# First attention block: a tile's values at the head of the following step, the residual behind the transposes, its bias three steps later

## The chip, the cores and the metric

One kernel runs on one core of one Trainium2 chip, as one launch. The metric is the device time of a launch in microseconds. All arithmetic is in float32. PE is the matrix engine, DVE, ACT and POOL are the vector, scalar and general engines, SP issues the DMAs. PE, DVE, ACT and POOL each take their instructions strictly in the order in which the program records them. The order on SP is set by the framework.

## What is computed

Four stages follow each other, each with a layer norm ahead of it and a residual around it: an attention block with windows of 64 keys (stage A, the one that is changed), two layers of local attention with gated FFNs (stage B), a gated attention unit (stage C) and a ternary linear layer. The input is 2 sequences of 2048 tokens with 256 features. Cut to the changed stage:

```python
def _L0_attn_ref(x, ...):            # 16 query heads, 4 key heads, 16 features a head
    h = _layernorm(x, g1, b1)
    q, k, v = heads(h @ Wq + bq), heads(h @ Wk + bk), heads(h @ Wv + bv)
    q, k = _rope(q), _rope(k)
    scores = einsum(q, k) / sqrt(16)
    valid = (col <= row) & (row - col < 64)
    attn = softmax(where(valid, scores, -1e9))
    out = einsum(attn, v)
    x = x + (out @ Wo + bo)
    h2 = _layernorm(x, g2, b2)
    return x + gelu(h2 @ Wf1 + bf1) @ Wf2 + bf2

x = x + _L0_attn_ref(_layernorm(x), ...)
```

The block gets a normalised x, and normalises it again. So each row has two scales from one variance: rs[0] gives the block's input, which is its residual y, and rs[1] gives the twice normalised rows h.

## The kernel before

The 4096 rows are 32 tiles of 128, and four tiles are a group (GT = 4, eight groups). Stage A is a pipeline over steps: in step s tile s is projected, tile s-1 gets its scores, the weights of tile s-2 are transposed and multiplied with the values, and tile s-3 is multiplied with Wo and added to its residual. A table (`at(step, what, ...)`) says which step does what for which tile or group, and `step_a` writes the instructions of a step in an order set by hand; every engine keeps that order.

In a full step PE does, in this order: the scores of tile s-1 (L446, 64 small matmuls), the projection of tile s (L380), a piece of the FFN of an earlier group (`fill(0)`: L552 for hidden columns, L563 for output tiles), the transposes of the rotated queries and keys of tile s (L427, L428), the transposes of the weights of tile s-2 (L476), the second FFN piece (`fill(1)`), the values of tile s-2 (L496) with their row sums (L503), the output of tile s-3 (L518), and, in two of four steps, the eight transposes of a group of normalised rows (`transposed`, L215, copied by ACT in L220). Steps without FFN pieces (up to step 7, and some at the end) have the transposes of the weights ahead of L427.

DVE follows: the mask is added to the scores in four pieces (L456, `mask(0)` to `mask(3)`), between them come the bias of the projection (L389), the cosine product (L411) and the sums of the rotation (L416, L421), then the row maxima (L465, two halves), the sums of the FFN output pieces (L570), statistics (L145, L146), normalised rows (L170 for the attention, L198 for the FFN and for the stage's result), the reciprocal of the row sums and the product (L512, L513, `take_values`), and the residual sum (L524, `add_output`). POOL copies the values of the tile to a padded array (L392), from which SP sends two DMAs to the arrays `vmid`; it makes the two sine products (L403, L406), subtracts the maxima (L466), raises variances to -1/2 (L161 for two scales at once, L137 for one) and adds bias rows (`add_rows`, L207). ACT makes the exponents (L469), copies transposes from PSUM (L433, L434, L436, L484, L220), makes y (L184) and applies gelu (L558).

The norm of group g is spread over steps: its x is loaded in step 4g-5, its statistics (`statistics_twice`) are made in step 4g-3, its `normalise` in step 4g-2. `normalise` writes h on DVE, then y on ACT (`normalised_once`), and adds bo to y on POOL. The FFN norm of a group (`prepare`) stands in step 4g+7. Each PSUM tile takes one of eight banks. `statistics_twice` also serves the rows of stage C.

The lines of the step that the change moves, as they stand:

```python
        if e:
            e.last_normalise()
        if a:
            a.values()
            a.take_values()
        if o:
            o.output()
            o.add_output()
        if q:
            q.exponents()
```

Here `a` is tile s-2, `o` tile s-3, `q` tile s-1, `p` tile s; `m` is the group in its `normalise`, `f` the one in `prepare`, `e` the one that is finished.

Of the kernel before, what the change touches and what calls it, by code (L numbers as in the profile page):

```python
# [12 lines left out]
ALU = mybir.AluOpType  # L13
# [8 lines left out]
GT = 4  # L22
# [23 lines left out]
def kernel(ctx: ExitStack, tc: tile.TileContext, I: dict, out: bass.AP):  # L46
    nc = tc.nc
    uid = [0]

    def T(pool, shape, tag, bufs=None):  # L50
        uid[0] += 1
        kw = {} if bufs is None else {"bufs": bufs}
        return pool.tile(shape, F32, tag=tag, name=f"{tag}_{uid[0]}", **kw)
# [18 lines left out]
    mhalf = T(const, [P, 2 * BH], "mhalf")  # L72
# [67 lines left out]
    def means_of(src):  # L140

        mv = T(small, [P, GT, 2], "mv")
        for t in range(GT):
            st = T(small, [P, 6], "st")
            nc.vector.bn_stats(st, src[:, t, :])  # L145
            nc.vector.bn_aggr(mv[:, t, :], st)  # L146
        return mv

    def statistics_twice(src):

        mv = means_of(src)
        ve = T(small, [P, 2, GT], "ve2")
        nc.vector.tensor_scalar_add(ve[:, 0, :], mv[:, :, 1], EPS)
        nc.vector.tensor_scalar(ve[:, 1, :], mv[:, :, 1], 1.0 + EPS, EPS * EPS, ALU.mult, ALU.add)
        rs = T(small, [P, 2, GT], "rs2")  # L160
        nc.gpsimd.tensor_tensor(  # L161
            rs, ve, mhalf[:, 0 : 2 * GT].rearrange("p (a b) -> p a b", a=2), ALU.pow
        )
        return mv, rs

    def normalised_twice(src, stats, dst):

        mv, rs = stats
        for t in range(GT):
            nc.vector.tensor_scalar(  # L170
                dst[:, t, :], src[:, t, :], mv[:, t, 0:1], rs[:, 1, t : t + 1], ALU.subtract, ALU.mult
            )

    def normalised_once(src, stats, dst, residual):

        mv, rs = stats
        scale = rs[:, 0, :]
        shift = T(small, [P, GT], "sh2")
        nc.vector.scalar_tensor_tensor(shift, mv[:, :, 0], -1.0, scale, ALU.mult, ALU.mult)
        if residual:  # L180
            scale = T(small, [P, GT], "sc2")
            nc.vector.tensor_scalar_add(scale, rs[:, 0, :], 1.0)
        for t in range(GT):
            nc.scalar.activation(  # L184
                dst[:, t, :], src[:, t, :], AF.Identity,
                bias=shift[:, t : t + 1], scale=scale[:, t : t + 1],
            )
# [17 lines left out]
    def add_rows(dst, rows):  # L205
        for t in range(GT):
            nc.gpsimd.tensor_add(dst[:, t, :], dst[:, t, :], rows(t))  # L207
# [18 lines left out]
    def load_qkv(l):  # L226
        w = {}
        w["wqkv"] = T(wB, [P, KC, 3 * BIN], "wqkvB")
        load(w["wqkv"], I["L0_ffn_wqkv"][l].rearrange("(k p) n -> p k n", p=P))
        return w  # L230

    def load_wo(l):
        w = {}
        w["wo"] = T(wB, [P, BIN // P, D], "woB")
        load(w["wo"], I["L0_ffn_wo"][l].rearrange("(k p) n -> p k n", p=P))
        return w
# [42 lines left out]
    class GroupA:  # L279
# [7 lines left out]
        def statistics(self):  # L287
            self.stats = statistics_twice(self.xg)

        def normalise(self):  # L290
            self.h = T(wa, [P, GT, D], "h", 1)
            normalised_twice(self.xg, self.stats, self.h)
            self.y = T(wa, [P, GT, D], f"y{self.g % 3}", 1)
            normalised_once(self.xg, self.stats, self.y, residual=False)
            add_rows(self.y, lambda t: boA)

        def to_features(self):
# [287 lines left out]
    def at(step, what, *args):  # L585
        steps.setdefault(step, {}).setdefault(what, []).append(args)
# [6 lines left out]
    for g in range(NG):  # L593
        at(GT * g - 5, "load", g)
        at(GT * g - 3, "statistics", g)
        at(GT * g - 2, "normalise", g)
        s = GT * (g + 1) + 3
        at(s - 1, "residual", g)
        at(s, "prepare", g)

        if g < NG - 1:
            for c in range(ADFF // P):
                at(s + 1 + c // 4, f"fill{c // 2 % 2}", g, "hidden", c)
            for tt in range(GT):
                at(s + 3 + tt // 2, f"fill{tt % 2}", g, "output", tt)
        at(s + 5, "finish", g)

    groups_a, tiles_a, ffns_a = {0: first_group}, {}, {}
    steps_a = steps

    def step_a(todo):
        p = a = q = o = n = m = f = e = None
        for (g,) in todo.get("load", ()):
            if g:
                groups_a[g] = GroupA(g)
        if "project" in todo:
            (t,) = todo["project"][0]
            if t == GT:
                weights.update({**load_qkv(0), **load_wo(0), **load_ffn(0)})
            p = tiles_a[t] = TileA(t, groups_a[t // GT])  # L620
        if "scores" in todo:
            q = tiles_a[todo["scores"][0][0]]
        if "attend" in todo:
            a = tiles_a[todo["attend"][0][0]]
        if "output" in todo:
            o = tiles_a.pop(todo["output"][0][0])
        for (g,) in todo.get("residual", ()):
            ffns_a[g] = FfnA(groups_a[g])
        if "statistics" in todo:
            n = groups_a[todo["statistics"][0][0]]  # L630
        if "normalise" in todo:
            m = groups_a[todo["normalise"][0][0]]
        if "prepare" in todo:
            f = ffns_a[todo["prepare"][0][0]]
        if "finish" in todo:
            e = ffns_a.pop(todo["finish"][0][0])

        def fill(place):

            rest = []  # L640
            for g, what, i in todo.get(f"fill{place}", ()):
                x = ffns_a[g]
                if what == "hidden":
                    rest.append(lambda x=x, i=i, r=x.hidden(i): x.take_hidden(i, r))
                else:
                    rest.append(lambda x=x, i=i, r=x.output(i): x.take_output(i, r))
            return rest

        if q:
            q.scores()  # L650
            q.mask(0)
            q.mask(1)
        if p:
            p.project()
            p.take()
        if q:
            q.mask(2)
        if p:
            p.rotate()
        if q:  # L660
            q.maxima(0)
            q.mask(3)
            q.maxima(1)
        pieces = fill(0)
        if a and not pieces:
            a.weights_to_keys()
            a.take_weights()
        for r in pieces:
            r()
        if n:  # L670
            n.statistics()
        if f:
            f.statistics()
        if e:
            e.last_statistics()
        if p:
            p.to_features()
            p.take_features()
        if a and pieces:
            a.weights_to_keys()  # L680
            a.take_weights()
        for r in fill(1):
            r()
        if m:
            m.normalise()
        if f:
            f.normalise()
        if e:
            e.last_normalise()
        if a:  # L690
            a.values()
            a.take_values()
        if o:
            o.output()
            o.add_output()
        if q:
            q.exponents()
        if m:
            m.to_features()
        if f:  # L700
            f.to_features()


    wC = Region(W_A, END)
# [16 lines left out]
    class RowsC:  # L721
# [5 lines left out]
        def statistics(self):  # L727
            self.stats = statistics_twice(self.R)
# [353 lines left out]
    class Ffn:  # L1082
# [45 lines left out]
        def residual(self):  # L1128
            Rg, w = self.Rg, self.w
            for tt in range(GT):  # L1130
                nc.gpsimd.tensor_add(Rg[:, tt, :], Rg[:, tt, :], w["b2"])
            if self.l == BL - 1:
                for tt in range(GT):
                    nc.gpsimd.tensor_add(Rg[:, tt, :], Rg[:, tt, :], self.xr[:, tt, :])
# [225 lines left out]
    head_c, bias = [rows[0].statistics, rows[0].normalise, rows[1].statistics], bias_c()  # L1360
# [3 lines left out]
    with tc.manual_schedule(engines=ENGINES):  # L1364
        for s in range(min(steps_a), JOINT + max(steps) + 1):
            if s in steps_a:
                step_a(steps_a[s])
            if GT < s < JOINT - 4:
                next(masks, None)
            if s == JOINT + s_a + 6:  # L1370
                nc.gpsimd.memset(hh[:, 5, :], 0.0)
            step_b(steps.get(s - JOINT, {}))
# [32 lines left out]
    class BatchC:  # L1405
# [14 lines left out]
        def rows(self, gl_):  # L1420
            return rows[self.b * GPS + gl_]
# [292 lines left out]
```

## Time and profile before

| | |
|---|---|
| median of 3 runs | 2669.41 us (2669.31 to 2669.52) |
| profiled execution | 2669.28 us, span 2667.1 us |
| PE busy | 2598.4 us (97%) |
| DVE busy | 1608.5 us (60%) |
| ACT busy | 1198.5 us (45%) |
| POOL busy | 992.6 us (37%) |
| granted PE clock | 0.991 of full speed |

The profile is one execution. An instruction's record has its engine, line, operation, the tiles it writes and reads, its start and length; an idle time before it is put down to the event that ended it. Matmuls are pipelined, so a busy PE need not be at its peak. Nearly every tile lies in one large array that the program calls `room`; a bank of PSUM is called `ps`. "Step 2" and the like below are steps of stage A; step 0 projects tile 0. Stage A takes the time up to about 510 us; its last group's FFN is mixed with the first steps of stage B.

### The profile page before, as it was taken

Reading aid. Unit: us, or ns where it says so; the run is one execution under the profiler, and the core shown is the slowest. Engines: PE = TensorE matmul, PEld = TensorE weight load, DVE = VectorE, ACT = ScalarE, POOL = GpSimd, SP = SyncE. Lnnn points to the kernel's source line nnn. Section 1 sums busy time; section 2 is a strip of 40 time slices with the busy share of each in tenths; the row PEclk is TensorE's granted clock in tenths of the full one; section 3 lists DMA queues with packets and bytes.
Section 4 is the critical chain, followed back from the end, with each engine's and each line's share of the span. In section 5 each row is a group of like instructions: output and inputs, shape, how many; then the busy total and the mean of one; then the engine's idle time right before and its main releaser. Section 6 shows DMA issues by size and latency. Waiting matters only on the chain.

```text
span 2667.1 us, 51195 instructions
## 1 busy us (share of the span) xinstructions
PE 2598.4 (97%) x20130; PEld 1644.4 (62%) x20130; DVE 1608.5 (60%) x4357; ACT 1198.5 (45%) x2505; POOL 992.6 (37%) x1221
## 2 busy tenths in 40 slices
PE   6899999999999999999999999999999999999998
PEld 4577777566666666666666666666544445445567
DVE  6777777468666666756766666674434344434344
ACT  3555555366666666646666666663510001500000
POOL 5655555445444444433644544442200001300011
PEclk8999999999999999999999999999999999999999
DMA  5011110111100011111211111101100000100000
GB/s 169 17 31 32 31 48 26 43 37 47 25 21 21 25 29 25 49 27 39 78 29 25 29 33 35 27 17 57 29 19 4 6 7 12 44 0 6 4 10 12
DMA packets 73166, 82.00 MB, mean 31 GB/s; under 512 B 18829, under 2 KB 57056, under 8 KB 72672
## 3 DMA queue, kind: packets, MB, share of 16 engines
q1 hardware_dynamic: 72928, 78.75, 10.6%
q8 instruction: 159, 2.61, 0.4%
q14 instruction: 79, 0.65, 0.1%
HBM read 44.20 MB, written 10.50 MB: 21 GB/s over the span
## 4 chain that ended last, share of the span: by engine, by line
PE 91%; DVE 5%; POOL 2%; DMA 1%; issue 1%; SPq 0%; ACT 0%; DVEq 0%; ACTq 0%; POOLq 0%
PE ps L1567 16%; PE ps L893 12%; PE ps L1147 10%; PE ps L1170 6%; PE ps L1491 4%; PE ps L552 4%; PE ps L563 4%; PE ps L1075 4%; PE ps L968 3%; PE ps L1046 3%; PE ps L1510 2%; PE ps L1479 2%; PE ps L949 2%; PE ps L1018 2%; PE ps L1469 2%; PE ps L476 2%
## 5 line engine op out<-in xcount | busy, mean ns | idle before, releaser
L1567 PE MATMUL ps<-room 128*128 128x512 f32 (+1 forms) x1152 | 463.2, 544 | 0.0
L893 PE MATMUL ps<-room 128*128 128x512 f32 x768 | 364.0, 610 | 0.0
L1567 PEld LDWEIGHTS ps<-room 128*128 128x128 f32 x1152 | 217.8, 189 | 221.9 <-issue 214.7
L999 ACT ACTIVATE room<-room,shift,rn 128x192 f32<-128x192 f32 x512 | 275.5, 543 | 79.6 <-DVE shift L987 78.7
L914 POOL TENSOR_TENSOR room<-room 128x256 f32<-128x256 f32 x128 | 115.8, 905 | 473.6 <-ACT room L905 472.0
L1147 PE MATMUL ps<-room 128*128 128x512 f32 x640 | 287.7, 593 | 0.4 <-ACT room L220 0.4
L1535 ACT COPY room<-ps 128x256 f32<-128x256 f32 x32 | 11.8, 370 | 587.9 <-PE ps L1533 587.9
L932 POOL TENSOR_TENSOR rn<-ss,mhalf 128x8 f32<-128x8 f32 x128 | 243.6, 1903 | 10.7
L893 PEld LDWEIGHTS ps<-room 128*128 128x128 f32 x768 | 135.9, 190 | 132.3 <-issue 117.7
L1497 DVE SCALAR_TENSOR_TENSOR room<-ps,room 128x512 f32<-128x512 f32 (+1 forms) x144 | 90.2, 627 | 206.4 <-PE ps L1491 206.4
L1147 PEld LDWEIGHTS ps<-room 128*128 128x128 f32 x640 | 118.8, 190 | 136.8 <-issue 122.7
L980 DVE CUSTOM_DVE_ANT_0 room<-ps,room 128x192 f32<-128x192 f32 x512 | 152.2, 353 | 66.7 <-PE ps L968 66.7
L1520 POOL TENSOR_SCALAR veC<-mvC 128x1 f32<-128x1 f32 x32 | 7.2, 224 | 453.5 <-DVE mvC L1518 453.5
L1170 PE MATMUL ps<-room 128*128 128x256 f32 x768 | 175.0, 382 | 0.0
L1170 PEld LDWEIGHTS ps<-room 128*128 128x128 f32 x768 | 145.2, 192 | 25.4 <-issue 6.7
L1010 DVE TENSOR_SCALAR room<-room,rdB 128x192 f32<-128x192 f32 x512 | 154.4, 366 | 4.5
L1163 DVE SCALAR_TENSOR_TENSOR room<-ps,room 128x512 f32<-128x512 f32 x96 | 72.1, 751 | 122.4 <-PE ps L1147 87.2
L466 POOL TENSOR_TENSOR room<-room,mxA 128x1024 f32<-128x1024 f32 x64 | 120.2, 1898 | 58.5 <-PE ps L428 45.4
L1491 PE MATMUL ps<-room 128*128 128x512 f32 (+1 forms) x288 | 133.4, 545 | 0.0
L968 PEld LDWEIGHTS ps<-room 64*64 64x64 f32 x4096 | 98.5, 134 | 48.4 <-ACT room L907 30.3
L937 DVE TENSOR_TENSOR room<-room 128x512 f32<-128x512 f32 x128 | 87.9, 687 | 63.1 <-ACT room L905 63.1
L1075 PE MATMUL ps<-room 128*128 128x256 f32 x512 | 120.9, 379 | 0.0
(182 smaller groups left out, 5008.7 us busy)
## 6 DMA issues: line engine op xcount, KB each, us to landing
room<-room SPq DMA_DIRECT2D x144, 128.0 KB
room<-in_L_attn_x_dram SPq DMA_DIRECT2D x16, 512.0 KB
room<-in_rope_b_dram SPq DMA_DIRECT2D x16, 512.0 KB
xs<-room SPq DMA_DIRECT2D x8, 512.0 KB
room<-xs SPq DMA_DIRECT2D x8, 512.0 KB
room<-in_rope_c_dram SPq DMA_DIRECT2D x8, 512.0 KB
out_dram<-R SPq DMA_DIRECT2D x32, 128.0 KB
room<-in_L_ffn_w_dram SPq DMA_DIRECT2D x6, 640.0 KB
```

What stands on the lines that cost most here:

```text
L466: nc.gpsimd.tensor_sub(Sh, Sh, mc.unsqueeze(2).to_broadcast([P, 2 * AG, P]))
L893: nc.tensor.matmul(pm, src[:, cols], self.w["wqkv"][:, k, part * BIN : (part + 1) * BIN], start=k == 0, stop=k == 1,)
L932: nc.gpsimd.tensor_tensor(self.rn[part], ss, mhalf[:, 0:BH], ALU.pow)
L968: nc.tensor.matmul(sc[e][q, jj * KW + c0 : jj * KW + c0 + n], self.qkT[0][rows, j, q], keys[b][part][rows, j, :], start=True, stop=True,)
L980: nc.vector.tensor_tensor_reduce(S[:, e, jj, :], sc[e][:, jj * KW : (jj + 1) * KW], self.mask[:, jj, :], 1.0, -3.0e38, ALU.add, ALU.max, t ...
L999: nc.scalar.activation(S[:, e, jj, :], S[:, e, jj, :], AF.Exp, bias=self.shift[half][:, a : a + 1], scale=self.rn[0][:, head : head + 1], ...
L1010: nc.vector.tensor_scalar_mul(S[:, e, jj, :], S[:, e, jj, :], rd[:, a : a + 1])
L1075: nc.tensor.matmul(pm[:, 0:D], self.oT[:, k, :], wo[:, k, :], start=k == 0, stop=k == BIN // P - 1)
L1147: nc.tensor.matmul(pm, w["w1"][:, k, half, c * P : (c + 1) * P], hT[:, k, :], start=k == 0, stop=k == KC - 1,)
L1170: nc.tensor.matmul(pm[:, 0:D], hh[:, c, tt * P : (tt + 1) * P], self.w["w2"][:, c, :], start=c == 0, stop=c == BNC - 1,)
L1491: nc.tensor.matmul(pm[:, 0:n], self.KT[:, J * P : (J + 1) * P], self.QT[:, q0 : q0 + n], start=True, stop=True,)
L1567: nc.tensor.matmul(acc[e][:, 0:n], self.V[:, J, e * P : (e + 1) * P], s2, start=J == 0, stop=J == TPS - 1,)
```

## The change

The power of `statistics_twice` becomes two instructions, the scale of h first. A tile's values and `take_values` leave the end of step t+2 and stand at the head of step t+3, ahead of the scores of the next tile; the output of the same tile stays near the end of step t+3. `normalise` keeps only h; y is made in a function `residual` behind the transposes of h, at the end of the same step; bo is added in `add_bias` at the end of step 4g+1, three steps later.

```diff
-        nc.gpsimd.tensor_tensor(
-            rs, ve, mhalf[:, 0 : 2 * GT].rearrange("p (a b) -> p a b", a=2), ALU.pow
-        )
+        for a in (1, 0):
+            nc.gpsimd.tensor_tensor(rs[:, a, :], ve[:, a, :], mhalf[:, 0:GT], ALU.pow)
...
         def normalise(self):
             self.h = T(wa, [P, GT, D], "h", 1)
             normalised_twice(self.xg, self.stats, self.h)
+
+        def residual(self):
             self.y = T(wa, [P, GT, D], f"y{self.g % 3}", 1)
             normalised_once(self.xg, self.stats, self.y, residual=False)
+
+        def add_bias(self):
             add_rows(self.y, lambda t: boA)
...
         at(GT * g - 2, "normalise", g)
+        at(GT * g + 1, "bias", g)
...
+        if o:
+            o.values()
+            o.take_values()
         if q:
             q.scores()
...
-        if a:
-            a.values()
-            a.take_values()
         if o:
             o.output()
             o.add_output()
...
         if m:
             m.to_features()
+            m.residual()
         if f:
             f.to_features()
+        for (g,) in todo.get("bias", ()):
+            groups_a[g].add_bias()
```

## The prediction

> **What bounds the kernel now.** I read the stretches by stage first, then the order of instructions at the start, then two steady steps of the first attention block. In the stretches the columns are the stretch, its length, busy time (and instructions) of PE, weight load, DVE, ACT and POOL, the granted clock of PE, the DMA share and GB/s.
>
> ```profile
> 0.00:21.50 21.50, 6.00 (x18) 3.21 (x18) 5.44 (x19) 5.56 (x10) 11.95 (x38) 0.99 0.66 188
> 21.50:104.40 82.90, 64.97 (x939) 44.38 (x940) 72.05 (x127) 39.09 (x65) 51.31 (x56) 0.89 0.34 98
> 104.40:468.70 364.30, 364.30 (x4057) 261.03 (x4062) 280.81 (x544) 200.89 (x305) 199.01 (x227) 1.00 0.11 32
> 468.70:546.00 77.30, 68.31 (x463) 42.39 (x466) 38.16 (x98) 35.92 (x64) 36.68 (x47) 0.96 0.13 40
> ```
>
> The block runs to about 469 us. From step 8 (104.4 us) to its last projection PE never waits: 364.30 of 364.30. There a change can take nothing away from PE's wait, it can only add one. Before that, DVE is busy 72.05 of 82.90 us and PE waits for it; the start is a chain of single waits. So a gain has room only in the first 104 us.
>
> The start, by the timeline (start, length, engine, line, then in brackets the idle time and what ended it):
>
> ```profile
> 13.43 1.43 ACT L220 ACTIVATE room<-ps,room 128x512 f32<-128x512 f32 x2
> 14.24 2.93 PE L380 MATMUL ps<-room 128*128 128x384 f32 x4 [2.85 <-ACT room L220]
> 15.22 2.77 POOL L207 TENSOR_TENSOR room<-room 128x256 f32<-128x256 f32 x4 [6.56 <-DMA room<-in_L_attn_bo_dram]
> ...
> 17.93 0.50 POOL L392 COPY room<-room 128x64 f32<-128x64 f32 x1
> ...
> 19.90 0.66 PE L427 MATMUL ps<-ident,room 128*128 128x128 f32 x4 [2.74 <-DVE room L416]
> ```
>
> Two things delay tile 0: ACT makes y (L184, with its table load 10.15 to 13.5) ahead of the two copies of the transposes (L220), and POOL waits for bo and adds it (until 17.99) ahead of L392.
>
> A steady step, and the tail of the next one:
>
> ```profile
> 255.17 1.76 DVE L512 RECIPROCAL room<-ps 128x256 f32<-128x256 f32 x1 [2.94 <-PE ps L503]
> 256.10 1.21 PE L446 MATMUL ps<-room 32*64 32x128 f32 x64
> 257.24 1.56 PE L380 MATMUL ps<-room 128*128 128x384 f32 x4
> 257.64 1.28 DVE L456 TENSOR_TENSOR room<-ps,room 128x512 f32<-128x512 f32 x2
> 258.84 0.55 DVE L389 TENSOR_TENSOR room<-ps,room 128x384 f32<-128x384 f32 x1
> 261.00 0.43 DVE L416 TENSOR_TENSOR room<-room 128x256 f32<-128x256 f32 x1 [0.48 <-POOL room L406]
> 262.08 0.60 PE L427 MATMUL ps<-ident,room 128*128 128x128 f32 x4
> ```
>
> ```profile
> 283.04 1.04 POOL L137 TENSOR_TENSOR rs<-ve,mhalf 128x4 f32<-128x4 f32 x1
> 283.56 1.08 PE L496 MATMUL ps<-room 128*32 128x128 f32 x32
> 284.11 2.21 DVE L198 TENSOR_SCALAR room<-room,mv,rs 128x256 f32<-128x256 f32 x4
> 285.43 1.13 PE L518 MATMUL ps<-room 128*128 128x256 f32 x4
> 286.40 1.04 PE L215 MATMUL ps<-ident,room 128*128 128x128 f32 x8
> ```
>
> PE is the bound, but with little to spare. In the first, L416 and L421 hand over at about 261.5 and PE comes to L427 at 262.08: half a microsecond. In the second, the last normalised row of L198 is there at 286.3, and PE comes to its transposes (L215) at 286.40, only because the values (L496, L503: 283.56 to 285.43) and the output (L518) lie between the last fill piece and L215. The change takes the values away from that place.
>
> **The change part by part.** Times are relative to the profiled execution (2669.28 us, span 2667.1; the median of the runs is 0.1 above it). V is the start of the scores.
>
> *1. Start: a gain of 3.9 us.* The power is split: a 128x4 power takes 1.04 us (L137), the 128x8 one 1.66 (L161), so h starts 0.6 earlier, transposes at 8.5 instead of 9.09. ACT's first work is now the table load and the copies: the first copy ends at about 10.4, not 14.2, the projection ends at 13.4, DVE's L389 comes at 13.4, not 17.20, POOL's L392 at 14.0, not 17.93, since bo's addition is gone from there. The weights and tables this needs were asked for by 6.8 us and carry about 1.4 MB, which the queue had moved by some 10 us by its GB/s over time. L427 of tile 0: about 16.0 instead of 19.90.
>
> *2. The bias three steps later: it takes this back.* add_bias stands at the end of step 1, on POOL behind both L466 and the power and ahead of step 2's L392. The group's x is asked for at 24.43 on SP and lands some 3.6 us later as the first one did (0.72 to 4.33), so its statistics begin at 28.2, end at 30.6; two powers until 32.8, four additions of 0.70 (2.77 in all) until 35.6: L392 of step 2 at 35.6, where it stood before (35.70). Net of 1 and 2: -0.1. In step 5 the same order delays step 6's L392: POOL's power ends at m+11.6 (m: first mask of step 5), the bias at m+14.4, L392 would be due at m+13.7: +0.7. In steps 9, 13 and on POOL has 2 us to spare and the bias costs nothing; if that cover were gone it would be 2.8 us each. The residual itself (2.08 us of ACT) lies behind the copies, where ACT is idle until the next L433; the x load on SP waits for it and goes out some 2.6 us later, still ahead of the step's vmid loads and two steps ahead of its statistics: nothing.
>
> *3. Values at the head, before the fill pieces start.* Before, the values of step 2 ran before the transposes that wait for DVE (41.3 to 44.4); now behind them, and DVE's reciprocal, product and first mask behind those: V+0.14 for the reciprocal, +1.79, +0.35, so the first mask at V+2.28, and V itself 1.87 later. L389 of step 3 at 50.9 instead of 48.79: +2.1. Steps 3 and 4: the reciprocal could start when DVE was free (6.82 after the first mask); now PE reaches the values behind L427 (3.92), L428 and the output (to 5.66) and ends them at 7.53, the period is 7.67+2.13 = 9.80 instead of 9.28: +1.0 for two. Step 5: +0.2, and the 0.7 of the bias. Step 6 waits for L170 (84.64 to 87.6) with nothing left to do meanwhile, values behind it: first mask at 92.4 instead of 90.09, +2.3. Step 7, the same behind L198: +2.1 (3.4 if PE's clock is at half there). Sum of the part before step 8: -0.1+2.1+1.0+0.9+2.3+2.1 = +8.3 us.
>
> *4. Steps 8 to 31, every step: L427.* First mask at V+2.28, two masks 1.20, so L389 at V+3.48 (before: V+2.74, held by the projection). From L389 to PE's L427 is 2.74 where PE waits (58.07 to 60.81), so V+6.22; PE arrives at V+5.98 (256.10 to 262.08). A wait of 0.24, and L427 with L428 takes 0.66 when it starts from a wait (60.81 to 61.47) against 0.55 in the flow: 0.35 a step, 24 steps: +8.4.
>
> *5. Six steps with an FFN normalisation (11, 15 ... 31).* T is the end of the second fill piece (283.56). DVE's chain is 0.75 later against V and PE's 0.35 at most, so the power (L137) ends at about T+1.0 instead of T+0.5; L198 then takes 2.21 (0.61 a row beside POOL's additions, where a row alone takes 0.41): last row at T+3.3. PE, without the values in between, arrives at T+0.97 and would want that row at T+1.3. +2.0 each: +12.0. If the power were as early as before, 1.4 each.
>
> *6. Five steps with an attention normalisation (10, 14 ... 26).* L170 runs from T+0.45, last row at T+1.9; PE wants it at T+1.3: +0.6 each, +3.0.
>
> *7. PE's clock.* No gap of this kind is in the trace after step 8. The nearest row is step 6:
>
> ```profile
> 79.00:82.40 3.40, 0.88 (x8) 0.53 (x5) 2.88 (x7) 1.01 (x3) 1.51 (x3) 1.00 0.12 29
> 82.40:85.80 3.40, 3.40 (x49) 2.26 (x48) 3.37 (x5) 0.87 (x3) 2.76 (x2) 0.52 0.00 0
> ```
>
> One gap of 2.5 us in a stretch of 3.4 and the clock of the next 3.4 is half. [...] By the trace the stalls of part 5 (four short ones, 2 us within 2.3) may be enough when they fall into one stretch, a third of them by the lengths: two of six, 1.7 us each. I go with the row but weight it down to +2, keep 0 and +10 as ends.
>
> *8. The split power in the third block's rows* costs POOL 0.4 us for each of eight groups, h comes 0.6 earlier; POOL is busy 87.69 of the last 767 us. 0, within 1 either way: the scale of y comes 0.4 later, and nothing waits for y at once.
>
> Sum: 8.3+8.4+12.0+3.0+2.0 = +33.7 us on 2669.3: 2703.
>
> **The rivals.** *A: the stalls of 5 and 6 are half as long*, because POOL's power stays early and L198 runs at its 0.41 a row. For it: L198 on R takes 1.38 for four. Against: the additions of bf2 (L207) follow each row at once and stay. It would save some 10 us: 2690, 2683 to 2695. *B: the clock.* All six stalls and the waits of the first steps halve the clock behind them: 2703+8 to +12, so 2713. [...] *C: faster.* The start is on the path that ends everything, since PE is full after step 8: 3.9 us gained there would be kept if add_bias of step 1 found POOL free and the waits at L427 did not arise. The point is 3.9 us over 24 steps, 0.16 us a step: DVE's half microsecond at L427 would have to bear the shift of 0.75, and DVE would have to overtake the transposes of the six steps. Then 2665.5, and a few us less where DVE's waits of the first steps shrink too. Against it: the half microsecond is measured, and L198 cannot start before the fill piece that DVE drains ahead of it. *D: the pieces cancel*, 2669 within 5.
>
> **How the numbers follow.** All stalls as summed: 0.65, own range 2695 to 2710. A: 0.16. B: 0.10. C: 0.06. D: 0.03. The range of 2685 to 2714 takes in the first, most of A and half of B. About 0.2% (5.3 us) is what a measurement of this kernel tells from no change: faster 0.03 (the half of C beyond 2664), same 0.06 (the other half, and D), slower 0.91.
>
> **What would show it.** Right: L392 of tile 0 near 14 and L427 near 16 us; no gain left at step 2's L392 (35 to 36 us); from step 8 on PE waits at L427 for DVE in each step, 0.2 to 0.4 us, and at the FFN transposes for L198, about 2 us, every fourth step; the four-step period 60.70 us grows to about 64.7; PE is no longer 100% busy between step 8 and the end of the block. The time behind the block (from 501 us of before) only moves. Wrong: a period that stays within 1 us of 60.70 would leave C or D; PE at half clock in more than two of the six stalls, B.

## The result, and the profile after

The changed kernel takes 2706.17 us in the median of 4 runs (2704.05 to 2707.8), beside 2669.36 us (4 runs) of the kernel before on the same chip: a ratio of 1.0137, 95% interval 1.012 to 1.0155. Its profiled execution took 2707.8 us with a span of 2705.7. The forecast was 2703.0, range 2685 to 2714, slower with 0.91.

The stretches of the changed kernel, by the same cuts as before (stretch, length, busy time and instructions of PE, weight load, DVE, ACT, POOL, then PE's clock, DMA share, GB/s):

```profile
0.00:21.50 21.50, 9.60 (x83) 5.99 (x84) 6.56 (x21) 5.67 (x10) 9.74 (x35) 1.00 0.64 188
21.50:104.40 82.90, 58.26 (x808) 40.34 (x808) 61.70 (x107) 34.70 (x58) 41.71 (x47) 0.81 0.33 97
104.40:468.70 364.30, 347.71 (x3704) 240.44 (x3703) 265.65 (x520) 192.22 (x291) 193.57 (x226) 0.97 0.10 31
468.70:546.00 77.30, 75.77 (x718) 55.38 (x717) 42.73 (x81) 32.25 (x45) 30.35 (x35) 1.00 0.05 17
```

In the first stretch PE already does 83 matmuls where it did 18: the start is faster. In the second it does 808 in place of 939, at a clock of 0.81 in place of 0.89: the gain is gone and more. In the third PE was full and now is not (347.71 of 364.30), and the clock, 1.00 before, is 0.97. The last is longer filled because the block ends later.

Because totals of one kernel scatter by some 2 us (before: 2666.8 to 2671.8 over all runs of the study), I follow one landmark through the block: the start of DVE's addition of the projection bias (L389 before, L392 after), once per step. It is read from one execution of each kernel, and ahead of step 8 it scatters as well: at step 7, up to which their programs are the same, the changed kernel stands at +12.16 and three of the variants below (PE kept busy, and the two that move POOL's additions) at +11.04, +10.59 and +10.43. From step 8 on, steps without a stall repeat within 0.1 us.

| L392 after minus L389 before, us | step 0 | 2 | 3 | 6 | 7 | 8 | 31 |
|---|---|---|---|---|---|---|---|
| changed kernel | -3.45 | +0.58 | +6.49 | +7.15 | +12.16 | +15.60 | +37.00 |

The span grew by 38.6, so 1.6 came behind step 31, the last FFN stall among it. Of the 37.0, 15.6 arise before step 8 and 21.4 from there on. The waits of PE name the places (who waits, for what, us in total, times, longest). The whole run; the last of these lines as it was in the kernel before; then 112 to 500 us of the changed kernel alone:

```profile
PE ps L214 <- DVE room L197: 16.8, 24, 5.5
PE ps L214 <- DVE room L169: 14.0, 5, 8.5
...
PE ps L430 <- DVE room L424: 12.9, 6, 5.2
```

```profile
PE ps L427 <- DVE room L421: 4.7, 5, 2.5
```

```profile
PE ps L214 <- DVE room L197: 13.4, 18, 5.5
```

L214 are the transposes of normalised rows (L197 for the FFN, L169 for attention; 8.5 of the latter is the start of the program). L430, the transposes of the rotated tile, waits for 12.9 us in place of 4.7; all six waits counted there lie ahead of step 8. In the steady part the list holds nothing else than the FFN's: three waits in each of six steps, 7 to 27 (the 5.5 is step 7's).

A steady step of the changed kernel, by the timeline; V, the start of the scores (L449), is 134.91:

```profile
134.91 1.21 PE L449 MATMUL ps<-room 32*64 32x128 f32 x64
135.04 1.76 DVE L515 RECIPROCAL room<-ps 128x256 f32<-128x256 f32 x1 [1.48 <-PE ps L506]
...
137.18 1.28 DVE L459 TENSOR_TENSOR room<-ps,room 128x512 f32<-128x512 f32 x2
138.37 0.55 DVE L392 TENSOR_TENSOR room<-ps,room 128x384 f32<-128x384 f32 x1
...
141.12 0.63 PE L430 MATMUL ps<-ident,room 128*128 128x128 f32 x4
```

Reciprocal at V+0.13, masks at V+2.27, L392 at V+3.46, L430 at V+6.21: each within 0.02 of the forecast. An FFN step (step 11):

```profile
178.15 1.03 PE L521 MATMUL ps<-room 128*128 128x256 f32 x4
178.21 1.04 POOL L137 TENSOR_TENSOR rs<-ve,mhalf 128x4 f32<-128x4 f32 x1
...
179.28 2.20 DVE L197 TENSOR_SCALAR room<-room,mv,rs 128x256 f32<-128x256 f32 x4 [0.51 <-POOL rs L137]
179.78 5.71 POOL L206 TENSOR_TENSOR room<-room 128x256 f32<-128x256 f32 x8 [0.53 <-DVE room L197]
...
179.84 0.56 PE L214 MATMUL ps<-ident,room 128*128 128x128 f32 x2 [0.67 <-DVE room L197]
...
180.81 0.33 PE L214 MATMUL ps<-ident,room 128*128 128x128 f32 x1 [0.40 <-DVE room L197]
...
181.53 0.92 PE L214 MATMUL ps<-ident,room 128*128 128x128 f32 x5 [0.40 <-DVE room L197]
...
182.38 1.94 PE L499 MATMUL ps<-room 128*32 128x128 f32 x32
```

The rows of L197 come one by one and PE takes each as it comes. The values behind them take 1.94 us, not 1.08: PE runs at half clock just after the stall (0.50 granted from 182.00 to 185.42). That is so behind steps 11, 19 and 27; behind 15 and 23 the same stall leaves the clock at full (1.00 in the 3.41 us that follow).

### The profile page after: what moved, and what is told of

Same layout as the page of the kernel before. It is cut to its first block, busy times and chain, and to the rows that moved or that the text cites. A ratio compares the mean times of both kernels' runs of the same rounds, so it can differ in the third digit from the quotient of the medians.

```text
span 2705.7 us, 51206 instructions
## 1 busy us (share of the span) xinstructions
PE 2618.1 (97%) x20130; PEld 1652.3 (61%) x20130; DVE 1609.2 (59%) x4357; ACT 1201.0 (44%) x2505; POOL 999.0 (37%) x1237
## 4 chain that ended last, share of the span: by engine, by line
PE 86%; DVE 8%; POOL 4%; issue 1%; DMA 0%; ACT 0%; SPq 0%; POOLq 0%; DVEq 0%; ACTq 0%
PE ps L1574 16%; PE ps L900 12%; PE ps L1154 10%; PE ps L1177 6%; PE ps L1498 4%; PE ps L1082 4%; PE ps L975 3%; PE ps L555 3%; PE ps L1053 2%; PE ps L566 2%; PE ps L1517 2%; PE ps L1486 2%; PE ps L956 2%; PE ps L1025 2%; PE ps L1476 2%; PE ps L214 2%
```

## The experiments

In the first four the question is which part of the change costs what. Theory V: the moved values make the loss alone, and the start's gain and the bias in step 1 cancel. Theory B: the bias in step 1, with slow clock behind it, makes a third of what is lost ahead of step 8.

**The moved values alone**, on the kernel before:

```diff
+        if o:
+            o.values()
+            o.take_values()
         if q:
             q.scores()
...
-        if a:
-            a.values()
-            a.take_values()
```

> The kernel before with one edit: values and take_values of a tile at the head of the next step; power, residual and bias as before. Theory V (the moved values make the loss alone; the start gains 3.5 us and the bias in step 1 takes the same back): 2706, within 2, first L389 at 17.2 and the pairs of halved clock behind steps 11, 19, 27 as in the changed kernel. Theory B (the bias in step 1, with the slow clock behind it, makes a third of the 15.6 us lost ahead of step 8): 2700 to 2702, since no bias stands ahead of step 2's vo copy on POOL here.

Measured: 2703.70 us, ratio 1.0131 (1.0114 to 1.0148). It lies between the two. By the landmark, +11.34 at step 8 and +32.62 at step 31: from step 8 on the same 21.3 as the change, ahead of it 4.3 less, although it has no gain at the start. V holds from step 8 on, B ahead of it, in direction more than in size: at step 7 this run stands at +7.89, which is 4.3 below the changed kernel and 2.5 to 3.2 below the three variants that repeat it up to there. The totals alone do not separate this run from the change, since their intervals overlap. The granted clock from 104.4 to 468.7 us is 0.97, as in the changed kernel.

**The values back**, on the changed kernel (`a.values()` and `a.take_values()` at their old place, the rest of the change kept):

> The changed kernel with values and take_values back at the end of step t+2; split power, residual behind the transposes and bias at step 4g+1 stay. Theory V: start -3.5, bias in step 1 +3.6, step 5 to 6 +0.7: 2670, within 1.5, and PE busy without a wait from step 8 to the end of the block. Theory B: the copy of step 2 on POOL waits to 39.3, PE runs at half clock behind it: 2673 to 2676.

Measured: 2669.49 us, ratio 1.0002 (0.9994 to 1.0011). The landmark is at -3.28 in step 0, +0.53 in step 3, +2.25 in step 8 and +2.26 in step 31. So the residual, the bias and the power together give 3.3 us, take them back ahead of step 8 (5.5 in this execution), and cost nothing from there on. The total shows no change, as V had it, where B's was 2673 to 2676. That the landmark ends at +2.26 is of the size of its scatter: with x alone, below, it ends at +2.31, with the same total as before.

**The bias one step sooner**, with the values at the head and with the values back:

```diff
-        at(GT * g + 1, "bias", g)
+        at(GT * g, "bias", g)
```

> The changed kernel with add_bias at the end of step 4g instead of 4g+1, so for the first group ahead of the power of group 1 on POOL. Theory V: the copy of step 2 is at 35 to 36 again instead of 39.3: 2706 - 3.6 = 2702.5. Theory B: the slow clock of steps 2 and 3 goes as well: 2697 to 2700. A third: bo lands at about 15.2 and x of group 1 at 32 whatever POOL does, and the projection of step 3 waits for DVE anyway: 2706, no change.

> The changed kernel with both undone or mended: values at the end of step t+2, add_bias at the end of step 4g; split power and residual behind the transposes stay. If the gain of the start is kept (PE is full from step 8 on, so what comes earlier stays earlier): 2669.4 - 3.5 = 2666. If it is lost ahead of step 8 (x of group 1 is asked for later, since its buffer is read by the residual until later, and lands after 31 us): 2669 to 2670.

Measured: 2703.28 us, ratio 1.0129 (1.0114 to 1.0144), and 2671.76 us, ratio 1.0008 (1.0002 to 1.0015). With the values at the head the landmark at step 3 falls from +6.49 to +2.13, at step 8 from +15.60 to +10.18: B's third again (3.7 to 5.4 us at step 7, against the same four runs). The total is nearer to V's 2702.5 than to B's 2697 to 2700, because the edit costs later: at the end of step 12, 16 and so on, POOL comes to the next step's first copy late, since the additions of 2.8 us run into it; +0.7 a group net with the values back, +1.2 with them at the head (where the granted clock from 130 to 500 us is 1.00, for 0.99 in the changed kernel, which hides it in the total). Step 4g+1 was the free place in the steady part, as the prediction had it, and the wrong one for the first group. With the values back, the start's -3.22 is at -0.12 by step 2 even without a bias in step 1. Something else holds step 2.

It is the x of group 1, as the run that asks for it sooner will show. The changed kernel, by the timeline (SPq is SP's queue):

```profile
25.30 0.38 SPq L56 DMA_DIRECT2D room<-in_L_attn_x_dram  x1
...
32.05 0.43 DVE L145 BATCH_NORM_STATS2 st<-room 128x6 f32<-128x256 f32 x1 [3.78 <-DMA room<-in_L_attn_x_dram]
...
34.63 1.99 POOL L162 TENSOR_TENSOR rs<-ve,mhalf 128x4 f32<-128x4 f32 x2 [4.39 <-DVE ve L159]
35.66 0.55 DVE L392 TENSOR_TENSOR room<-ps,room 128x384 f32<-128x384 f32 x1
36.59 2.77 POOL L206 TENSOR_TENSOR room<-room 128x256 f32<-128x256 f32 x4
39.30 0.24 POOL L395 COPY room<-room 128x64 f32<-128x64 f32 x1
...
40.52 0.42 DVE L419 TENSOR_TENSOR room<-room 128x256 f32<-128x256 f32 x1 [3.19 <-POOL room L409]
```

DVE waits 3.78 us for x, which lands 6.75 us after it was asked for; its statistics stand ahead of step 2's masks on DVE, so the masks wait as well, to 34.46. The power follows, then the bias, and only at 39.30 the copy that stood at 35.70 before.

**Values by step**, and PE kept busy, on the changed kernel. The first puts the values at the end in the steps of a normalisation, the second gives PE something to do in the stall:

```diff
-        if o:
+        if o and not o.valued:
             o.values()
             o.take_values()
...
+        if a and (m or f):
+            a.values()
+            a.take_values()
+            a.valued = True
         if o:
             o.output()
```

```diff
         if f:
+            fz = bank4()
+            for i in range(16):
+                nc.tensor.transpose(fz[:, i % GT, :], ident, ident)
             f.to_features()
```

> The changed kernel, but in the steps that normalise a group (4g+2) or prepare an FFN (4g+3) the tile's values stand at the end again, ahead of the output and of the transposes; in the other steps at the head of the next. If the loss is PE waiting at the transposes because the values no longer lie between (parts 5 and 6, with the halved clock behind three of them, and the same in steps 6 and 7): the 21 us lost from step 8 on and some 7 us of steps 6 and 7 come back, 2677 to 2680. If the wait at the rotated tile's transposes in every step is the larger share, as the prediction's 8.4 us against 15 would put it: 2684 to 2686. If the slow start (bias, steps 2 and 3) is the larger: above 2690.

> The changed kernel with 16 transposes of the identity into a bank of their own, which nobody reads, ahead of the FFN's transposes: PE is busy while it would wait for the normalised rows, and nothing else changes. If the halved clock behind the stalls of steps 11, 19 and 27 comes from the stalls: it is gone, 3 x 1.6 = 4.9 us less, 2701.5, less up to 2 more in step 7, and the period of these steps 17.9 in place of 19.6 us. If the clock falls for another reason: 2706, and the transposes add up to 0.2 us each: 2707.

Measured: 2671.12 us, ratio 1.0008 (1.0001 to 1.0014). The landmark is at +2.89 in step 8 and +3.75 in step 31: 33 of the 37 us are gone with the values back in half of the steps. That is below all three forecasts: ahead of step 8 not some 7 us came back but 12.7. The stalls at the transposes are the loss; the head place in the other steps costs 0.9 us from step 8 on.

And 2698.68 us, ratio 1.0117 (1.01 to 1.0134). The stretch around the stall of step 11 with the 16 transposes:

```profile
176.88:180.29 3.41, 3.25 (x25) 2.84 (x23) 2.54 (x5) 1.36 (x1) 2.80 (x5) 1.00 0.38 154
180.29:183.70 3.41, 3.27 (x99) 2.52 (x104) 0.98 (x3) 2.73 (x3) 3.41 (x6) 1.00 0.00 0
```

From step 11 to 12 the landmark grows by 2.33, not 3.94; all five FFN steps from there on take 17.94 to 17.96 us, none the 19.6 of a halved clock, and the granted clock from 130 to 500 us is 1.00, for 0.99. From step 8 to 31 it grows by 16.5, not 21.4. Three times 1.6 us is the clock's share; the stall's own 2.3 stays. The filled time costs nothing that the trace shows.

**FFN rows without POOL's additions beside them** (rival A's cause), in two versions. The first, shown here, issues `add_rows` of bf2 and xr behind `f.to_features()`; the second three steps later, at the end of step 4g+10 for group g, the last group excepted:

```diff
             normalised(self.y, self.stats, self.h)
+
+        def add_rest(self):
             add_rows(self.y, lambda t: bf2)
             add_rows(self.xr, lambda t: self.y[:, t, :])
...
+            f.add_rest()
```

> The changed kernel with POOL's eight additions of an FFN group (bf2 to y, y to xr) issued behind the transposes of h instead of row by row beside the normalised rows. Rival A's cause: the rows take 0.61 us beside POOL's additions and 0.41 alone; then the last row is ready 0.6 us sooner in each of seven stalls, and the shorter stalls may keep the clock: -4 us, or -9 with the clock, 2697 to 2702. If POOL's additions do not slow the rows: L197 stays at 2.20 us for four, 2706, within 1.

> The changed kernel with the eight additions of an FFN group (bf2 to y, y to xr) issued three steps later, at the end of step 4g+6 of the same numbering, where POOL is idle for some 9 us; the last group keeps its place. The earlier run that only put them behind the transposes left them on POOL beside the rows, at the same time as before, so it did not try rival A's cause. Rival A's cause: the four normalised rows then take 1.5 us instead of 2.20, each stall of the FFN steps is some 0.6 us shorter (6 x 0.6 = 3.6), and PE's clock stays at full (3 x 1.6 = 4.8 more): 2698 to 2702. If POOL does not slow DVE's rows: L197 at 2.20 again, 2706 to 2707.

Measured: 2706.97 us, ratio 1.0142 (1.0127 to 1.0157), then 2702.13 us, ratio 1.0125 (1.0108 to 1.0142). In the first nothing moved: L206 stands behind PE's transposes in the program, but in step 11 it began at 178.17, ahead of the first of them (178.23) and 0.49 us after the first row, as before (0.50). The second does move them. Its additions read a y that group g+3 has replaced by then, so it adds other numbers; the instructions are the same in kind and number. The line of L197 (shortest, median and longest in ns), first of the changed kernel, then of this one, and this one's stall of step 11:

```profile
L197 DVE TENSOR_SCALAR room<-room,mv,rs x32: 405/610/822, 113.0 to 549.2; 128x256 f32<-128x256 f32 x32
```

```profile
L197 DVE TENSOR_SCALAR room<-room,mv,rs x32: 394/407/816, 111.3 to 543.7; 128x256 f32<-128x256 f32 x32
```

```profile
176.87 1.38 DVE L197 TENSOR_SCALAR room<-room,mv,rs 128x256 f32<-128x256 f32 x4 [0.51 <-POOL rs L137]
...
177.43 1.64 PE L214 MATMUL ps<-ident,room 128*128 128x128 f32 x8 [0.67 <-DVE room L197]
```

610 ns beside the additions, 407 alone: rival A's cause is shown. The four rows take 1.38 us, the stall is 0.8 shorter, and behind it the values take 1.08 us, as at full clock; the five FFN steps from 11 on take 18.2 to 18.7 us, where the changed kernel's take 17.9 or, with the clock halved, 19.6. But the additions now run from 162.20 to 168.0 on POOL, over step 11's copy, and L430 waits 1.42 us for them there (8.3 us in six such waits from 104.4 to 500 us), which takes most of it back.

**Reciprocal and product later**, on the changed kernel:

```diff
         if o:
             o.values()
+        if o and f:
             o.take_values()
...
             q.maxima(1)
+        if o and not f:
+            o.take_values()
         pieces = fill(0)
```

> The changed kernel with take_values (reciprocal and product, 2.1 us of DVE) behind the second reduction of the maxima instead of ahead of the masks, except in the steps that prepare an FFN. If DVE's reciprocal and product ahead of the masks are what makes L430 wait 0.24 us a step (part 4): L430 finds its tile ready, the periods of 14.79 us fall to 14.55, below the 14.72 of before, about 18 x 0.23 = 4.1 us less from step 8 on and 1 to 2 less before: 2700 to 2701. If L430 waits for the projection or for POOL's rotation: 2706.

Measured: 2719.75 us, ratio 1.0192 (1.0177 to 1.0208), outside both forecasts, for a reason ahead of step 8. There are no fill pieces there, PE comes to the output (L521) at once, and waits for the product. PE's waits in 21.5 to 112 us:

```profile
PE ps L521 <- DVE room L516: 18.2, 4, 4.6
```

By the landmark +31.33 at step 8. In the steady part the expectation holds for the steps without an FFN stall: such a step is 14.53 us in place of 14.79, L430 stands at V+5.97 without a wait, and steps 8 to 10 lose nothing but gain 0.2 each on the kernel before. But here all five FFN steps between 8 and 31 take 19.5 to 19.6 us, as three of them do in the changed kernel, where the clock falls (17.9 where it does not), and the granted clock from 104.4 to 468.7 us is 0.96 for 0.97: by these lengths all five stalls halve it, not three. So from step 8 to 31 21.1 us are lost, hardly less than the 21.4 of the change, and the 4.1 that the expectation gave did not come.

**The x of group 1 asked for sooner**, with the values back and the bias at the end of step 4g+2, then alone on the kernel before. The twelve loads of scales of the later stage, which stood ahead of it on SP, go behind step 6:

```diff
-    scales = [load_scales(l) for l in range(BL)]
+    scales = []
...
                 step_a(steps_a[s])
+            if s == GT + 2:
+                scales.extend(load_scales(l) for l in range(BL))
```

> The changed kernel with values at the end of step t+2, add_bias at the end of step 4g+2, and the third stage's and second stage's q and k scales loaded after step 6 of the first block, so that the x of group 1 is asked for on SP ahead of those twelve loads. If the start's gain of 3.3 us was lost at step 2 because x of group 1 landed at 31 to 32 us and DVE's statistics stand ahead of the masks: L392 of step 2 near 32 instead of 35, the gain kept, 2666. If PE's half clock in the first steps takes it back: 2668 to 2669.5.

> The kernel before with that one edit alone: the scales loaded after step 6, x of group 1 asked for sooner. If x of group 1 is only late once the start is faster: 2669.4, no change within 0.5, the statistics of step 1 not sooner than DVE is done with the maxima. If it was already late before: up to 1 us less.

Measured: 2667.88 us, ratio 0.9995 (0.9987 to 1.0003), and 2669.60 us, ratio 1.0000 (0.9992 to 1.0008). x is asked for at 17.71, and DVE no longer waits for it:

```profile
28.45 0.42 DVE L145 BATCH_NORM_STATS2 st<-room 128x6 f32<-128x256 f32 x1
...
32.47 0.56 DVE L392 TENSOR_TENSOR room<-ps,room 128x384 f32<-128x384 f32 x1 [0.34 <-PE ps L383]
```

L392 of step 2 stands at 32.47 in place of 35.08, and 1.9 of the gain last until step 6. Then steps 6 to 8 take 1.8 of it (0.8 up to step 7, 1.0 from there). Alone, the edit gains nothing: x was not late for the slower start. Both expectations were right about step 2. What takes the 1.8 was not shown.

**Both findings together**: the values back, the bias at the end of step 4g+2 and x sooner, as above, and from tile 8 on the values of the tiles 4g+2 and 4g+3 at the head of the next step, reciprocal and product behind the maxima. (The expectation names the tiles 4g and 4g+1; by the edit these keep their place at the end of a step, since that step normalises.)

```diff
+        head = o and not o.valued
+        if head:
+            o.values()
...
             q.maxima(1)
+        if head:
+            o.take_values()
...
+        if a and (m or f or a.t < 8):
+            a.values()
+            a.take_values()
+            a.valued = True
```

> As the run with values back, bias at 4g+2 and x sooner, but from tile 8 on the values of tiles 4g and 4g+1 stand at the head of the next step, with their reciprocal and product behind the maxima. By the run that took them later the step is 0.2 us shorter than before there (14.53 against 14.72): twice in each of six groups, 2.4 us less than without it, 2663.5. If the mixed order gives it back in the steps between, as it did with the reciprocal ahead of the masks: 2666.

Measured: 2666.46 us, ratio 0.9991 (0.9983 to 0.9999), the fastest kernel of the study, by 2.9 us of 2669.36. The landmark falls by 0.4 us a group, from -0.91 in step 12 to -3.08 in step 31: these 2.2 us are the new order's, near the 2.4 expected; the 0.8 by which it stands below the run without it (-0.13) in step 12 already are scatter. The gain is below the 0.2% that the prediction called measurable; the landmark, not the total, carries the reading.

## Why the prediction was right, point by point

*1, the start.* -3.9 forecast for L427 of tile 0 (16.0); L430 came at 16.40 and L392 at 13.75, -3.45. Right.

*2, the bias.* -0.1 forecast at step 2's copy, +3.6 measured (39.30 for 35.70). The step that failed is "its statistics begin at 28.2": x was taken to land 3.6 us after being asked for, as the first load had, and took 6.75. In that time the DMA engines moved 157 GB/s, about 1.06 MB by my estimate, and x is 0.5 MB of it: other transfers were under way. That they held x up is likely, not shown. The trace of before gave a warning, no more:

```profile
24.43 0.38 SPq L56 DMA_DIRECT2D room<-in_L_attn_x_dram  x1
31.18 0.42 DVE L145 BATCH_NORM_STATS2 st<-room 128x6 f32<-128x256 f32 x1
```

DVE came to the statistics from the maxima just then and did not wait, so x may have landed at any time up to 31.18. That leaves room for anything up to 6.75 us; the prediction took 3.6 from the first load. Everything behind it was in the right order (statistics, two powers, four additions, copy) and 3.6 late. For step 5 the forecast was +0.7; in the run with the values back, step 6's copy comes at 81.12 for 79.64, of which 0.9 reach step 7.

*3, the values ahead of step 8.* +8.3 with parts 1 and 2, +15.6 measured. The moved values alone made +11.3 (7.7 forecast), the bias the rest, 2.5 to 4.3 by the scatter. Steps 3 and 4 were about right (+0.67 for +1.0). Steps 2, 6 and 7 were too small: +5.9, +5.0 and +3.4 for 2.1, 2.3 and 2.1; of step 2's, 3.2 are the bias, since it is 2.7 where the values alone are moved. In each of the three the values now run behind the wait and at half clock: 1.94 us for L499 and 1.85 to 1.94 for L506, against 1.08 and 1.05. The prediction priced the delay at full clock, and kept 3.4 for step 7, which came, as an aside.

*4, L427 in each step.* The wait is there, V+6.21 for V+6.22. The list of PE's waits does not show it, because the fill piece ahead of it (L555) ends by the model only at 141.04, just before L430 at 141.12; the run with the reciprocal later does, where L430 comes at V+5.97. Its price was 0.35 a step and is 0.07: 14.79 us from V to V in place of 14.72. The step that failed is that nothing else of PE's step would change. The same instructions in the new order are 0.2 us shorter: from the second fill piece's start to the next instruction 3.43 us with the output behind it (3.53 with the values before), and to the scores 0.97 from the second half of the values (1.07 from the output). The run with the reciprocal later shows it without the wait: 14.53.

*5, six FFN stalls.* 2.0 each forecast; 2.24 measured in the two that keep the clock (2.31 less the 0.07 of part 4). The last row came 3.34 us after T, 3.3 forecast.

*6, attention normalisations.* 0.6 forecast, 0.83 with part 4's 0.07.

*7, the clock.* +2 forecast, two of six stalls at 1.7 by the row, weighted down toward 0. No run shows this weight or the 0; in the changed kernel three of the five stalls between steps 8 and 31 halve the clock, 1.6 each, +4.8, as shown by the run with PE filled. Going with the row was right; its weight was too low, and it left out the first steps (21.5 to 104.4 us), where the clock is 0.81 for 0.89.

*The sum from step 8 to 31:* 23 x 0.07 + 5 x 0.76 + 5 x 2.24 + 3 x 1.6 = 21.4, as measured; and 23.0 to the end of the run; forecast 25.4. Ahead of step 8, 15.6 for 8.3. So that the total was met is in part luck: a part that was too small stood beside one too large. The sign named for the steady part, a four-step period of about 64.7 us for 60.70, came: 64.0 where the clock stays (steps 12 to 16), 65.6 where it falls (8 to 12). Of the rivals, B came true for half of the stalls. A's cause exists, but the change leaves POOL's additions where they were. C would have been paid at L427 (0.07 a step, below its 0.16), and failed at step 2, where x and the bias took the start's gain, and at the transposes.

*8, the split power in the third block:* nothing of it can be seen; of the 1.6 us behind step 31 the last stall explains all, and the rest is within the scatter.

## What to carry over

An instruction that seems to have slack may be the cover of another engine's chain: here the values hid the wait for normalised rows, the FFN's and the attention's, and 33 of 37 us came with moving them from that place. The gain at the start lasted until the first shared wait (-3.45 us in step 0, +0.58 in step 2), so follow it to there (x of the next group, which landed 6.75 us after it was asked for, the first one 3.6) and read a landing from the trace at that time, not from the first load. And what was put behind an instruction of another engine in the program was not held by it: L206, put behind PE's transposes, began 0.06 us ahead of them.

## What was not expected of the hardware

In these stalls the half clock came behind a window of 3.41 us in which PE was idle for 1.47 us in three gaps, not behind one long gap. In the profiled execution of the changed kernel the clock changes at 25.00, 31.82, 38.64 and 52.30 us and so on to 441.42 and 444.84, always whole multiples of 3.41 us apart: a grid. Cut on that grid, the windows with the stalls of steps 11, 15 and 23 and one of step 7, each with the window that follows it:

```profile
178.59:182.00 3.41, 1.94 (x10) 1.06 (x9) 2.71 (x6) 0.86 (x2) 2.88 (x4) 1.00 0.37 154
182.00:185.42 3.42, 3.42 (x51) 2.24 (x49) 0.00 (x0) 2.63 (x3) 3.42 (x6) 0.50 0.02 5
243.44:246.86 3.42, 2.24 (x10) 1.26 (x8) 2.39 (x5) 1.54 (x1) 2.74 (x4) 1.00 0.37 153
246.86:250.27 3.41, 3.12 (x92) 2.37 (x96) 0.98 (x3) 2.73 (x3) 3.41 (x6) 1.00 0.02 5
373.15:376.56 3.41, 2.08 (x9) 1.12 (x7) 2.54 (x5) 1.38 (x1) 2.80 (x5) 1.00 0.38 154
376.56:379.97 3.41, 3.27 (x99) 2.52 (x104) 0.98 (x3) 2.73 (x3) 3.41 (x6) 1.00 0.02 5
103.50:106.91 3.41, 1.64 (x16) 1.43 (x14) 2.89 (x7) 2.01 (x4) 1.52 (x3) 1.00 0.11 27
106.91:110.32 3.41, 1.14 (x7) 0.68 (x5) 3.31 (x7) 0.87 (x3) 2.59 (x2) 1.00 0.01 2
```

PE busy for 1.94 us of the window of step 11: half clock in the next; 2.24 and 2.08 in steps 15 and 23: not. Steps 19 and 27 have 1.95 and 1.94 and are halved. The five stalls are alike; what differs is where they fall in the grid. Among them 57% busy was followed by half clock and 61% was not. This is no edge for everything: the window of step 7 has PE busy for 1.64 us, 48%, with one gap of 1.77, and the clock stays at 1.00 behind it. What counts besides the busy time is open. The longest gap in the five stalls is 0.67 us.

That PE's same instructions took 0.2 us a step less in the new order (14.53 us for 14.72, without a wait in either) was new too; why is not shown.
